# Adding x on TensorE in the attention that runs beside a causal convolution: identity product, ScalarE copy, VectorE scaling from the bank

## Chip, core and metric

The kernel runs on one core of a Trainium2 chip. The metric is the device time of one launch in microseconds. A core has TensorE (PE in the profile; PEld is its weight load), VectorE (DVE), ScalarE (ACT), GpSimd (POOL) and SyncE (SP), which only issues transfers here. Everything is in fp32, and each fp32 matmul of the program stands as two records in the trace.

## What is computed

The input x has 4 batches of 512 time steps with 128 x 64 = 8192 features each. Layer 0, cut to what matters here (`layernorm` runs over the 8192 features):

```python
xn = layernorm(x, ln_attn_g, ln_attn_b)
k, v, r = xn @ Wk, xn @ Wv, sigmoid(xn @ Wr)
states = scan(s -> decay * s + k_t * v_t)          # over time
x = x + (r * states) @ Wo                          # attention
xn = layernorm(x, ln_freq_g, ln_freq_b)
x = x + gelu(conv(xn, freq_W, 3 taps over the 128) + freq_b)
xn = layernorm(x, ln_time_g, ln_time_b)
to = causal_conv(xn, time_W, 3 taps over time, per feature) + time_b
x = x + layernorm(to, time_ln_g, time_ln_b)
x = x + gelu(x @ ffn_W1 + ffn_b1) @ ffn_W2 + ffn_b2
```

Layer 1 subtracts a moving average over time, takes 128 Fourier modes, mixes them by complex weights and adds the inverse transform to the average. The change does not touch it.

## The kernel before

Layer 0 keeps features on the 128 partitions and the 512 time steps along the free dimension. The 8192 features are 64 chunks of 128, taken in 32 pairs; nearly every tile of layer 0 is a pair, 128 x 2 x 512.

For one batch the steps are `project` (J), `scan` (Z), `attend_and_convolve` (A), `convolve_time` (C), `open_feed` (O) and `feed_forward` (F). Two batches run beside each other. The function `in_turn` advances two Python generators by hand-written shares and leads, and TensorE's order is exactly this program order (`manual_schedule` for TensorE). On the other engines a scheduler orders the instructions; each engine then takes its own list strictly in order. The pairs that matter are C of batch 0, 1, 2 beside A of batch 1, 2, 3. A of batch 0 runs beside J of batch 1.

Inside A, `attend(i)` handles pair i. It loads `xp` (x, transposed) and `wo_sb`, multiplies them with `rst` (r times the states) into the PSUM tile `a` (L487: two products of 64 rows, one for each chunk), adds xp to it on VectorE into `x1` (L489), and multiplies x1 by the row `rb` of reciprocal deviations into `z` (L493). `scaled` makes weights on ScalarE (L501). `convolve(i)`, which trails attend by two pairs, fills a PSUM tile `cv` (tags `c` and `m` in turn): the bias and the mean's term by four two-row products (L508), the neighbours in the convolution by up to four 64 x 64 products (L517), and the pair's own part by two full products (L522). Then come a gelu in place on ScalarE (L523), the sum with x1 on VectorE into `x2` (L525), a store of x2 by POOL (L526), and its square on ScalarE (L528). `add_up` sums x2 and the squares over the features on TensorE into `st` (L249, 32 columns each), three pairs behind attend. Tile `a` has one buffer of two banks, xp, x1 and wo_sb have three, z has four.

Inside C, for each pair, VectorE scales x2 (L580) and subtracts the mean's row into `xh` (L582), ScalarE makes the first tap and the bias (L585, one for each chunk), VectorE adds the other two taps (L589, four instructions), POOL fixes the first two columns (L593) and stores, ScalarE squares (L595), and `add_up` sums into `p` (also L249).

`ident` is a 128 x 128 identity that is there from the start, as the second operand of transposes.

Of the kernel before, what the change touches and what calls it, by code (L numbers as in the profile page):

```python
# [12 lines left out]
ALU = mybir.AluOpType  # L13
# [3 lines left out]
P = 128  # L17
T = 512
NF = 128
H = 64  # L20
# [59 lines left out]
def layer0(ctx, tc, dram, x, xt, vecs, wkvr, wo, wdec, wconv, fbias, w1, fb1, w2, fb2, x4):  # L80
# [4 lines left out]
    nc = tc.nc  # L85
# [17 lines left out]
    def two(pool, tag):  # L103
        return pool.tile([P, 2, SL], F32, tag=tag, name=tag)


    ident = const.tile([P, P], F32, name="ident")
# [40 lines left out]
    cgr = const.tile([P, NPR, H], F32, name="cgr")  # L148
# [9 lines left out]
    def neighbours(q, c):  # L158

        return (c - 1, q), (c + 1, 1 - q)  # L160

    def rows_of(q, d):

        return 1 - q if d < 0 else q
# [79 lines left out]
    def add_up(st, i, pair, squares, first, last):  # L244

        for j in range(2):
            for k, src in ((0, pair), (1, squares)):
                q = 2 * j + k
                nc.tensor.matmul(  # L249
                    st[32 * q : 32 * q + 32, :], lhsT=ones, rhs=src[:, j, :],  # L250
                    start=first, stop=last,
                )

    def finish(st, bank, tag):

        s_sb = rowp.tile([P, SL], F32, tag="s", name="s_sb")
        nc.scalar.copy(s_sb, st)
        yield CHAIN
        pm = bank()
        for t in range(NT):  # L260
            nc.tensor.matmul(
                pm[:, 2 * t : 2 * t + 2], lhsT=s_sb[:, t * P : (t + 1) * P], rhs=pick,
                start=True, stop=True,
            )
        me = tiny.tile([P, NT, 2], F32, tag=f"me{tag}", name="me")
        nc.vector.tensor_copy(me.rearrange("p t k -> p (t k)"), pm[:, 0 : 2 * NT])
        return me[:, :, 0], me[:, :, 1]

    def moments(mean, square, tag):

        var, rs, mrs = cols(f"var{tag}"), cols(f"rs{tag}"), cols(f"mrs{tag}")
        nc.vector.tensor_tensor(var, mean, mean, ALU.mult)
        nc.vector.tensor_tensor(var, square, var, ALU.subtract)
        rsqrt(rs, var)
        nc.vector.tensor_tensor(mrs, mean, rs, ALU.mult)
        return rs, mrs

    def rows(bank, a, b, names):
        both = rowp.tile([P, 2, SL], F32, tag=names, name=names)
        for k, col in enumerate((a, b)):  # L280
            pb = bank()
            spread(pb, col)
            nc.scalar.copy(both[:, k, :], pb)
            yield CHAIN
        return both[:, 0, :], both[:, 1, :]

    def pair_of(row):
        return row.unsqueeze(1).to_broadcast([P, 2, SL])

    def load_x(b, i):  # L290
        xp = fr.tile([P, 2, SL], F32, tag="xp", name="xp")
        nc.sync.dma_start(xp, xt[b, 2 * i : 2 * i + 2].rearrange("c p t -> p c t"))
        return xp

    def c_bank():
        return two(ps_c, "c")
# [174 lines left out]
    def attend_and_convolve(b):  # L471
        rst, rs, mrs = scanned.pop(b)
        rb, mb = yield from rows(of_a, rs, mrs, "rm")

        nc.vector.tensor_scalar(mb, mb, at_one[:, 1:2], at_one[:, 0:1], ALU.mult, ALU.add)
        st = ps_s.tile([P, SL], F32, tag="s", name="st")
        free_s[0] = False
        x1s, zs, ws, waiting = {}, {}, {}, {}

        def attend(i):  # L480
            xp = load_x(b, i)
            wo_sb = fr.tile([P, P], F32, tag="wo", name="wo_sb")
            nc.sync.dma_start(wo_sb, wo[:, i, :])
            at = two(ps_a, "a")
            for j in range(2):
                js = slice(j * S, (j + 1) * S)
                nc.tensor.matmul(at[:, j, :], lhsT=wo_sb[js, :], rhs=rst[js, :], start=True, stop=True)  # L487
            x1 = x1s[i] = fr.tile([P, 2, SL], F32, tag="x1", name="x1")
            nc.vector.tensor_tensor(x1, at, xp, ALU.add)  # L489
            z = fr.tile([P, 2, SL], F32, tag="z", name="z", bufs=4)  # L490
            for j in range(2):
                zs[2 * i + j] = z[:, j, :]
            nc.vector.tensor_tensor(z, x1, pair_of(rb), ALU.mult)  # L493

        def scaled(i):

            wcs = fr.tile([P, 2, P + H], F32, tag="wcs", name="wcs")
            for j in range(2):
                c = 2 * i + j
                ws[c] = wcs[:, j, :]  # L500
                nc.scalar.mul(wcs[:, j, :], wc_sb[:, i % 2, :], vec[:, G2, c : c + 1])  # L501

        def convolve(i):
            cv = c_bank() if i % 2 or held[0] else two(ps_m, "m")
            for h in range(2):
                for j in range(2):
                    q = 32 * (2 * h + j)
                    nc.tensor.matmul(  # L508
                        cv[h * H : (h + 1) * H, j, :], lhsT=cgr[q : q + 2, i, :], rhs=mb[q : q + 2, :],
                        start=True, stop=False,  # L510
                    )
            for j in range(2):
                c = 2 * i + j
                for n, h in neighbours(i % 2, c):
                    if 0 <= n < NCH:
                        rs = halves[rows_of(n // 2 % 2, n - c)]
                        nc.tensor.matmul(  # L517
                            cv[halves[h], j, :], lhsT=ws[n][rs, P:], rhs=zs[n][rs, :], start=False, stop=False
                        )
            for j in range(2):  # L520
                c = 2 * i + j
                nc.tensor.matmul(cv[:, j, :], lhsT=ws[c][:, 0:P], rhs=zs[c], start=False, stop=True)  # L522
            nc.scalar.activation(cv, cv, AF.Gelu_apprx_tanh)  # L523
            x2 = two(bk, "x2")
            nc.vector.tensor_tensor(x2, cv, x1s.pop(i), ALU.add)  # L525
            nc.gpsimd.dma_start(x2d[b][2 * i : 2 * i + 2].rearrange("c p t -> p c t"), x2)  # L526
            sq2 = bk.tile([P, 2, SL], F32, tag="sq", name="sq2")
            nc.scalar.activation(sq2, x2, AF.Square)  # L528
            for c in (2 * i - 2, 2 * i - 1):
                zs.pop(c, None)  # L530
                ws.pop(c, None)
            if i + 2 < NPR:
                scaled(i + 2)
            waiting[i] = x2, sq2

        for i in range(2):
            scaled(i)
        for i in range(NPR + 3):
            if i < NPR:
                attend(i)  # L540
                yield 1.0
            if 1 < i < NPR + 2:
                convolve(i - 2)
                yield 5.0
            if i > 2:
                add_up(st, i - 3, *waiting.pop(i - 3), i == 3, i == NPR + 2)
                yield 1.0
        begin[attend_and_convolve], free_s[0] = b + 1, True
        mean3, sq3 = yield from finish(st, of_a, 3)
        carried[b] = moments(mean3, sq3, 3)  # L550
# [503 lines left out]
```

## Time and profile before

| | |
|---|---|
| median of 3 runs | 3954.09 us (3950.18 to 3962.51) |
| profiled execution, its time and its span | 3956.46 us, 3954.4 us |
| busy: PE, PEld, DVE, ACT, POOL | 94%, 35%, 67%, 45%, 15% of the span |
| granted TensorE clock, mean | 0.974 |
| the three stretches of A beside C | about 588 to 860, 1285 to 1560, 1996 to 2285 us |
| DVE busy in them | 255.9, 262.6, 268.7 us |

How to read it: a group or timeline row names the line of the kernel, the engine, the operation and "output<-inputs" by tile names; tiles that share a name in the program share it there, so `x` in an attention row stands for xp, x1 or x2. The busy time of PE counts a matmul until its modelled end, so a PE that is "busy" can still be late for its next start. An idle time before an instruction is given with the instruction that ended it, its releaser.

### The profile page before, as it was taken

The page shows a single profiled execution, that of the slowest core. Times are in us where ns is not written, and L with a number is a line of the kernel's source. Part 1 is how long each engine was busy: PE and PEld are TensorE (multiplying, and loading weights), DVE is VectorE, ACT ScalarE, POOL GpSimd, SP SyncE. Part 2 cuts the span into 40 slices and gives each one's busy share as a digit, 9 for nine tenths or more (in the row PEclk, how much of TensorE's full clock was granted, in tenths as well). Part 3 has the DMA queues.
Part 4 walks back from the last instruction along what each step waited for, and adds up shares of the span by engine and source line. Part 5 has one row for each costly group of instructions (what it writes and reads, how often), then busy time and mean ns, then how long its engine had stood idle before and what let it go on. Part 6 is the DMA issues. An engine that isn't in the chain of part 4 may idle for free. (4 is left out here: it accounts for less than half of the span.)

```text
span 3954.4 us, 45957 instructions
## 1 busy us (share of the span) xinstructions
PE 3721.8 (94%) x16463; PEld 1373.1 (35%) x16463; DVE 2646.6 (67%) x3430; ACT 1761.0 (45%) x2460; POOL 580.8 (15%) x1038
## 2 busy tenths in 40 slices
PE   9989989889999899999999988999989999999999
PEld 4433322223333222333322232333322653326533
DVE  1145559985555898655589989955549357783577
ACT  2113335545556555455556578877752210022100
POOL 0000002220000222000022222100014200142000
PEclk9989989999999999999989999999989999999999
DMA  5367637776664677767567767745549469895597
GB/s 173 126 224 262 231 127 242 249 254 228 232 234 149 232 258 247 247 221 236 172 209 255 258 218 257 244 160 179 182 155 306 163 196 297 297 303 176 186 294 268
DMA packets 417466, 884.49 MB, mean 224 GB/s; under 512 B 35352, under 2 KB 85720, under 8 KB 413144
## 3 DMA queue, kind: packets, MB, share of 16 engines
q1 hardware_dynamic: 334848, 605.12, 47.1%
q0 software_dynamic: 79872, 274.77, 19.3%
q8 instruction: 131, 2.15, 0.2%
q10 hardware_dynamic: 2520, 1.67, 0.1%
q14 instruction: 95, 0.78, 0.1%
HBM read 612.93 MB, written 268.50 MB: 223 GB/s over the span
## 5 line engine op out<-in xcount | busy, mean ns | idle before, releaser
L650 PE MATMUL pa<-mid,w_sb 128*64 128x512 f32 x2048 | 499.9, 609 | 49.5 <-DVE x4t L655 49.3
L643 ACT ACTIVATE mid<-m,fb_sb 128x1024 f32<-128x1024 f32 x256 | 284.9, 1113 | 294.8 <-PE m L639 294.2
L655 DVE SCALAR_TENSOR_TENSOR x4t<-pa,fb_sb,x 128x512 f32<-128x512 f32 x252 | 188.0, 746 | 254.2 <-PE pa L650 254.1
L639 PE MATMUL m<-x,w_sb 64*128 64x512 f32 x1008 | 289.8, 648 | 1.4 <-ACT mid L643 0.9
L589 DVE SCALAR_TENSOR_TENSOR to<-xh,vec,to 128x512 f32<-128x512 f32 x384 | 277.2, 746 | 10.7 <-issue 6.8
L643 ACT ACTIVATE mid<-c,fb_sb 128x1024 f32<-128x1024 f32 x256 | 283.2, 1106 | 0.6 <-PE c L639 0.6
L639 PE MATMUL c<-x,w_sb 64*128 64x512 f32 x1008 | 262.4, 594 | 1.3 <-ACT mid L643 1.3
L650 PEld LDWEIGHTS pa<-mid,w_sb 128*64 128x64 f32 x2048 | 125.0, 136 | 392.7 <-issue 227.5
L361 PE MATMUL a<-xp,both 128*128 128x512 f32 x512 | 244.8, 605 | 6.4 <-DVE both L358 5.9
L249 PE MATMUL st<-x,ones 128*32 128x512 f32 x512 | 204.2, 613 | 35.3 <-DVE x L525 35.2
L922 PE MATMUL b<-xin,avg_sb 128*128 128x512 f32 x512 | 230.9, 593 | 3.0 <-DVE xin L928 3.0
L899 ACT COPY two<-a 128x512 f32<-128x512 f32 x64 | 37.5, 585 | 424.1 <-PE a L894 424.1
L358 DVE TENSOR_SCALAR both<-both,vec 128x192 f32<-128x192 f32 x192 | 53.3, 316 | 258.5 <-DMA both<-in_wkvr 208.5
L928 DVE TENSOR_TENSOR xin<-b,pm 128x512 f32<-128x512 f32 x256 | 159.1, 684 | 95.4 <-PE b L925 80.5
L675 POOL DMA_DIRECT2D x<-ob x64 | 48.9, 765 | 1056.3 <-ACT ob L671 986.5
L616 ACT ACTIVATE kd<-kd,vec 128x512 f32<-128x512 f32 x256 | 193.6, 809 | 4.3 <-DVE kd L608 4.2
L528 ACT ACTIVATE sq<-x 128x1024 f32<-128x1024 f32 x128 | 134.6, 1051 | 135.6 <-DVE x L525 135.3
L249 PE MATMUL st<-sq,ones 128*32 128x512 f32 x640 | 172.2, 615 | 21.0 <-ACT sq L528 20.0
L825 DVE TENSOR_TENSOR uv<-xin 128x1024 f32<-128x1024 f32 x128 | 156.1, 1225 | 49.8 <-PE a L839 32.0
L355 DVE BATCH_NORM_STATS2 stt<-both 128x6 f32<-128x512 f32 x192 | 124.4, 685 | 92.7 <-DMA both<-in_x 91.8
L487 PE MATMUL a<-rst,wo_sb 64*128 64x512 f32 x512 | 153.5, 678 | 34.7 <-DVE x L489 33.6
L595 ACT ACTIVATE sq<-to 128x1024 f32<-128x1024 f32 x96 | 101.3, 1055 | 188.9 <-POOL xh L581 183.4
(242 smaller groups left out, 6804.3 us busy)
## 6 DMA issues: line engine op xcount, KB each, us to landing
xp<-in_xt SPq DMA_DIRECT2D x256, 512.0 KB
xin<-x SPq DMA_DIRECT2D x128, 1024.0 KB
kx<-x SPq DMA_DIRECT2D x224, 512.0 KB
x<-x POOLq DMA_DIRECT2D x128, 512.0 KB, 4.7
kh<-to SPq DMA_DIRECT2D x128, 512.0 KB
x<-ob POOLq DMA_DIRECT2D x64, 1024.0 KB, 6.7
out<-xin POOLq DMA_DIRECT2D x64, 1024.0 KB, 7.3
both<-in_x SPq DMA_DIRECT2D x96, 512.0 KB
```

Source lines behind the costliest of these rows:

```text
L249: nc.tensor.matmul(st[32 * q : 32 * q + 32, :], lhsT=ones, rhs=src[:, j, :], start=first, stop=last,)
L361: nc.tensor.matmul(pa[:, k, :], lhsT=wq[:, j, k * P : (k + 1) * P], rhs=xp[:, j, :], start=first and j == 0, stop=last and j == 1,)
L487: nc.tensor.matmul(at[:, j, :], lhsT=wo_sb[js, :], rhs=rst[js, :], start=True, stop=True)
L589: nc.vector.scalar_tensor_tensor(to[:, j, :], xh[:, j, k : SL + k], vec[:, w, c], to[:, j, :], ALU.mult, ALU.add)
L616: tc.keep_in_program_order(nc.scalar.activation(d[:, j, :], d[:, j, :], AF.Identity, bias=vec[:, B4, c], scale=vec[:, G4, c]))
L639: nc.tensor.matmul(pm[:, h, :], lhsT=w1_sb[hs, m * P : (m + 1) * P], rhs=x3[hs, :], start=True, stop=True)
L643: nc.scalar.activation(mid, pm, AF.Gelu_apprx_tanh, bias=fb1_sb[:, m : m + 1])
L650: nc.tensor.matmul(pa[h * H : (h + 1) * H, :], lhsT=w2_sb[:, m, :], rhs=mid[:, h, :], start=(m == 0), stop=(m == 1),)
L655: nc.vector.scalar_tensor_tensor(x4t, pa, fb2_sb, x3s[c // 2][:, c % 2, :], ALU.add, ALU.add)
L825: nc.vector.tensor_tensor(t, xin[:, 0:2, :], xin[:, 2:4, :], op)
L922: nc.tensor.matmul(po[j], lhsT=avg_sb[:, j, :], rhs=xin[:, j, :], start=True, stop=False)
L928: nc.vector.tensor_tensor(by_n(xin[:, j, :]), by_n(po[j]), by_c(pm[j % 2][:, j // 2, :]), ALU.add)
```

## The change

For batches 1, 2 and 3, attend(i) no longer adds xp on VectorE. TensorE adds it: a product of the identity with xp is accumulated onto `a`, for each of the two chunks. ScalarE then copies the sum from PSUM into x1, and VectorE reads the sum from PSUM, not from x1, to make z. Batch 0 keeps the old form. For all batches, the order of products inside convolve is turned round: the pair's own part first, then the neighbours, then the bias.

```diff
-                nc.tensor.matmul(at[:, j, :], lhsT=wo_sb[js, :], rhs=rst[js, :], start=True, stop=True)
+                nc.tensor.matmul(at[:, j, :], lhsT=wo_sb[js, :], rhs=rst[js, :], start=True, stop=b == 0)
             x1 = x1s[i] = fr.tile([P, 2, SL], F32, tag="x1", name="x1")
-            nc.vector.tensor_tensor(x1, at, xp, ALU.add)
+            if b == 0:
+                nc.vector.tensor_tensor(x1, at, xp, ALU.add)
+                base = x1
+            else:
+
+                for j in range(2):
+                    nc.tensor.matmul(at[:, j, :], lhsT=ident, rhs=xp[:, j, :], start=False, stop=True)
+                nc.scalar.copy(x1, at)
+                base = at
             z = fr.tile([P, 2, SL], F32, tag="z", name="z", bufs=4)
             for j in range(2):
                 zs[2 * i + j] = z[:, j, :]
-            nc.vector.tensor_tensor(z, x1, pair_of(rb), ALU.mult)
+            nc.vector.tensor_tensor(z, base, pair_of(rb), ALU.mult)
...
             cv = c_bank() if i % 2 or held[0] else two(ps_m, "m")
-            for h in range(2):
-                for j in range(2):
-                    q = 32 * (2 * h + j)
-                    nc.tensor.matmul(
-                        cv[h * H : (h + 1) * H, j, :], lhsT=cgr[q : q + 2, i, :], rhs=mb[q : q + 2, :],
-                        start=True, stop=False,
-                    )
+            for j in range(2):
+                c = 2 * i + j
+                nc.tensor.matmul(cv[:, j, :], lhsT=ws[c][:, 0:P], rhs=zs[c], start=True, stop=False)
...
-            for j in range(2):
-                c = 2 * i + j
-                nc.tensor.matmul(cv[:, j, :], lhsT=ws[c][:, 0:P], rhs=zs[c], start=False, stop=True)
+            for h in range(2):
+                for j in range(2):
+                    q = 32 * (2 * h + j)
+                    nc.tensor.matmul(
+                        cv[h * H : (h + 1) * H, j, :], lhsT=cgr[q : q + 2, i, :], rhs=mb[q : q + 2, :],
+                        start=False, stop=True,
+                    )
```

## Prediction, made before the changed kernel ran

> **What bounds the kernel now.** I read the page's busy line first. PE is busy for 94% of the span, but a matmul record includes its pipelined tail, so this alone does not show that PE sets the pace where the change is made. The changed branch runs only where attention of batch b stands beside the causal convolution of batch b-1. The busy time by windows of three such stretches of 50 us (PE, PEld, DVE, ACT, POOL busy, then granted clock, DMA share, GB/s) says who does:
>
> ```profile
> core 0: us, PE busy (x) PEld busy (x) DVE busy (x) ACT busy (x) POOL busy (x), PEclk, DMA share, GB/s
> 1400.00:1450.00 50.00, 45.33 (x228) 10.81 (x220) 50.00 (x56) 30.24 (x42) 12.61 (x24) 1.00 0.74 249
> 1450.00:1500.00 50.00, 46.10 (x235) 11.14 (x233) 49.86 (x54) 28.11 (x39) 13.98 (x23) 1.00 0.81 268
> 1500.00:1550.00 50.00, 45.59 (x233) 10.46 (x229) 49.48 (x53) 29.63 (x41) 14.77 (x22) 1.00 0.77 259
> ```
>
> VectorE (DVE) is busy without a gap; ACT has 40% free. The groups of DVE, one row per line and form, give its bill for one pair of chunks:
>
> ```profile
> L589 DVE SCALAR_TENSOR_TENSOR to<-xh,vec,to 128x512 f32<-128x512 f32 x113 | 82.5, 746 | 3.8 <-issue 2.7 <-ACT to L585 0.8
> L582 DVE TENSOR_TENSOR xh<-kd,rm 128x1024 f32<-128x1024 f32 x30 | 36.6, 1220 | 0.3
> L580 DVE TENSOR_TENSOR kd<-kx,rm 128x1024 f32<-128x1024 f32 x30 | 36.6, 1219 | 0.1
> L493 DVE TENSOR_TENSOR z<-x,rm 128x1024 f32<-128x1024 f32 x27 | 32.9, 1219 | 0.0
> L489 DVE TENSOR_TENSOR x<-a,xp 128x1024 f32<-128x1024 f32 x27 | 32.9, 1219 | 0.0
> ```
>
> L489, L493, L525, L580, L582 at 1.22 us and four L589 at 0.746 make 6.10 + 2.98 = 9.08 us. The measured period agrees: 11 L489 in each 100 us, 9.09 us. So DVE sets it.
>
> What does PE need for a period if it waits for nothing? The timeline of PE where attention of batch 0 runs beside a projection shows the same groups back to back; the start of each less the start of the one before is its price (start, us, operation):
>
> ```profile
> 407.06 1.13 PE L487 MATMUL a<-rst,wo_sb 64*128 64x512 f32 x4
> 408.12 1.98 PE L361 MATMUL m<-xp,both 128*128 128x512 f32 x4
> 410.04 1.09 PE L508 MATMUL c<-rm,cgr 2*64 2x512 f32 x8
> 411.06 1.09 PE L517 MATMUL c<-z,wcs 64*64 64x512 f32 x8
> 412.07 1.98 PE L522 MATMUL c<-z,wcs 128*128 128x512 f32 x4
> 413.89 1.88 PE L361 MATMUL m<-xp,both 128*128 128x512 f32 x4
> 415.70 0.62 PE L249 MATMUL st<-x,ones 128*32 128x512 f32 x1
> ```
>
> L487 1.06, L508 1.02, L517 1.01, L522 1.82; the sums of one statistic (8 records of L249) 1.00, from the next start at 416.70. A full 128x128 pair of products (L361) costs 1.92 behind another array shape, 1.81 behind its own. With two statistics a period is 1.06 + 1.02 + 1.01 + 1.82 + 2.0 = 6.9 us, so PE has about 2.2 us of slack, spent in waits for DVE and ACT, as in this timeline (bracket: idle before, and its releaser):
>
> ```profile
> 1401.95 1.22 DVE L525 TENSOR_TENSOR x<-c,x 128x1024 f32<-128x1024 f32 x1
> ...
> 1403.20 1.06 ACT L528 ACTIVATE sq<-x 128x1024 f32<-128x1024 f32 x1 [3.63 <-DVE x L525]
> ...
> 1403.22 1.05 PE L249 MATMUL st<-x,ones 128*32 128x512 f32 x2 [0.83 <-DVE x L525]
> ```
>
> A hand-over costs little: L528 starts 0.03 us after L525 ends.
>
> **What the Trainium skill says.** (1) VectorE: DVE Perf Modes, "The perf-mode tier table": a fp32 tensor_tensor runs in the 1x tier from SBUF and PSUM alike. The trace agrees: L489 (one input in PSUM) and L493 (both in SBUF) both take 1.219 us, so the scaling costs the same when it reads the bank. (2) PSUM — Partial Sum Buffer, "Terms": two engines must not touch one bank and quadrant at once, "reads against reads included". So copy and scaling can't run together; no line of before has such a pair, but in the changed program as built the scaling waits for ScalarE. (3) TensorEngine Tiling (Array Packing), "Key Properties": a change of tiling mode drains TensorE. The trace fits: 1.92 against 1.81. (4) TensorE: Matmul & The Clock Gate, "What's actually happening": activity releases the half-rate clock, idling brings it back. The windows of before show clock 1.00 above, but 0.92 over the third such stage (1996 to 2285 us).
>
> **The change part by part**, for 3 batches x 32 = 96 pairs:
>
> - *Removed:* L489 on DVE, 1.22 us. DVE is left with 7.86 us a period.
> - *Added on PE:* two products of 128x128 with the identity, in four records: like L361 behind L487, 1.92 us. They wait for xp, which DVE waited for before; same loads, same queue order at the start, and xp is freed by PE.
> - *Added on ACT:* a copy of 128x1024 from PSUM. The same operation at L369 took 1.012 us. ACT goes from 1.00 + 1.06 + 0.80 + 1.60 + 1.05 = 5.5 to 6.5 us a period: no bound by its sum.
> - *Moved:* in convolve the product L522 comes first and the bias L508 last, for batch 0 too. The number of array-shape changes is the same where L361 stands on either side, and next to the identity product one is saved: 0 for batch 0, from -0.1 to +0.1 us elsewhere. No DMA, POOL work or buffer count changes.
>
> *PE's new period:* 1.06 + 1.92 + 1.82 + 1.02 + 1.01 + 1.85 to 2.0 for the two statistics (1.85 if adjacent, from 1413.76 to 1415.61 in the timeline) = 8.7 to 8.8; I take 8.75. It exceeds DVE's 7.86, so **PE becomes the bound** and the best gain is 9.08 - 8.75 = 0.33 us, not 1.22.
>
> *Waits in the changed order.* The scheduler orders DVE and ACT; I took these orders from the changed program as built. In about 56 of the 96 periods DVE runs x2 (old L525), the four causal multiply-adds, the shift (L582), then the scaling: 4.2 us between x2 and the scaling, in which ACT does the square, half of L585 and the copy. The loop through ACT (x2 1.22, square 1.06, L585 0.80, two multiply-adds 1.49, three DVE operations 3.66, hand-overs 0.1) is 8.3 us, under 8.75. These gain 0.33 x 56 = **-18 us**.
> In 6 periods x2 stands directly ahead of the next scaling, which waits for the copy, which waits in ACT's order behind the square, which waits for x2. Then DVE stands still through both: 7.86 + 1.06 + 1.01 + hand-overs 0.05 = 9.98, or 0.9 more than now: **+6**.
> In 9 periods ACT also has the other square (L595, 1.05) in the loop: 8.3 + 1.05 = 9.4, 0.3 more: **+3**.
> The other 25 are ramps and changes of order. At a stage's start three attends run ahead of the first convolution. Today bank a is free after L489 alone (L487 starts at 1285.17, 1289.45, 1291.90); afterwards it takes 3.0 on PE, 1.01 copy, 1.22 scaling, so 5.3 us each: two gaps of 5.3 against 6.7 in all is +4, and up to +13 at half clock (products 6.0 instead of 3.0). I take +8 x 3 stages = **+24**. Where attention runs alone (some 3 periods, not counting starts) PE already sets the pace, 541.32 - 535.31 = 6.0 us, and the 1.92 counts in full: **+6**.
> *Clock.* At clocks 0.98, 0.98, 0.92 over 272, 275 and 289 us, half speed covers about 11 + 11 + 46 = 68 us (a mean of 0.98 is 4% of the time at half), which PE's slack mostly hides now; a PE-bound stage would lose half, 34 us. But a busier PE should fall there less: bounds 0 to +34, I take **+5**.
>
> Sum: -18 + 6 + 3 + 24 + 6 + 5 = +26. The profiled execution is 3956.5 us, its span 3954.4; the median of the runs is 3954.1, 0.06% away, so I add to the median: **3980 us** (+0.65%).
>
> **Rivals.**
> - *A, forecast: PE takes over and ramps lose more than the steady part gains.* For it: the PE bill above. Against: the -18 is sure only if the clock holds. Its own range is 3966 to 4010. Chance 0.45.
> - *B, the serial hand-over rules most periods:* when a transfer or slow clock upsets the order, every period runs through x2, square, copy, scaling. 96 x 0.9 = +86, 4040. For it: ACT and DVE take their work strictly in order. Against: only 6 periods stand so by order. Chance 0.20.
> - *C, faster:* DVE frees PE from its waits and the ramps are covered by causal work that DVE now does ahead. Price: 96 x -0.33 = -32, so 3922; it decides if each stage's start costs under 2 us rather than 8 and the clock stays at 1. For it: DVE is at 50.00 of 50. Against: the PE floor allows no more. Chance 0.15.
> - *D, both cancel,* ramps near +4 and clock at 0: within 12 us. Chance 0.20. The copy or product not being issued is no case: both stand in the changed program's lists, 96 times.
>
> **How the numbers follow.** About 0.3% (12 us) is what a measurement of this kernel can tell from no change. C gives faster 0.15, D same 0.20, A and B slower 0.65. The range leaves the further half of C and of B's upper tail out: 3940 to 4040.
>
> **What would show it.** Right: in the three stages DVE has gaps ahead of the scaling and the copy, PE is near 8.7 us a period with hardly an idle time before L249, the copy is near 1.01 and the scaling near 1.22 us, the first three attends of a stage stand 5 us or more apart. Wrong: a period still at 9.1 with DVE full; an identity pair well under 1.9 us; periods of 10 us through most of a stage (B); starts no later than today (C).

## The result and the profile after

The changed kernel takes 3975.98 us (median of 4 runs, 3971.61 to 3981.31), the kernel before 3953.41 us beside it (4 runs). The ratio is 1.0054, 95% interval 1.0033 to 1.0075: slower by about half a per cent. The profiled execution took 3981.31 us, its span is 3979.5 us, 25.1 us longer than the span before.

The changed kernel has other line numbers: the scaling L493 is now L501, the copy is L496 and the identity product L495; in convolve the pair's own part is L515, the neighbours L521, the bias L527, the gelu L531, x2 L533 and its square L536; in the causal convolution L588, L590, L593, L597 and L603 stand for the old L580, L582, L585, L589 and L595. The layer 1 line L825 is L833. The kernels of the experiments shift these numbers again; there the tile names tell what a row is.

The busy line of the page after:

```profile
PE 3800.9 (96%) x16847; PEld 1428.1 (36%) x16847; DVE 2562.9 (64%) x3334; ACT 1859.9 (47%) x2556; POOL 600.4 (15%) x1038
```

The work moved as the diff says: VectorE lost 84 us of busy time, ScalarE got 99, PE got 79. The prices of the new operations, first copy and scaling by line (count; ns of the shortest, the median and the longest; first and last start), then the group of the identity product (busy us and mean ns of one record; idle before):

```profile
L496 ACT COPY x<-a x96: 986/993/1014, 562.5 to 2280.3; 128x1024 f32<-128x1024 f32 x96
L501 DVE TENSOR_TENSOR z<-a,rm x96: 1214/1218/1225, 563.6 to 2281.3; 128x1024 f32<-128x1024 f32 x96
...
L495 PE MATMUL a<-xp,ident 128*128 128x512 f32 x384 | 198.7, 642 | 0.0
```

The scaling costs the same from the bank, and PE was never idle ahead of the identity product, so it never waited for xp.

The busy time by windows of the three stretches of attention beside the causal convolution, as in the table of before:

```profile
core 0: us, PE busy (x) PEld busy (x) DVE busy (x) ACT busy (x) POOL busy (x), PEclk, DMA share, GB/s
588.00:862.00 274.00, 266.01 (x1360) 80.86 (x1357) 236.06 (x259) 191.91 (x251) 83.16 (x129) 0.99 0.72 245
1287.00:1575.00 288.00, 274.89 (x1350) 80.28 (x1352) 236.30 (x251) 188.25 (x248) 72.40 (x123) 0.99 0.70 238
2006.00:2300.00 294.00, 280.96 (x1400) 84.26 (x1398) 239.47 (x259) 196.73 (x251) 85.90 (x128) 0.97 0.69 239
```

PE is now the fullest engine (266.0 of 274 us in the first stage, against 242.5 of 272 before), VectorE has 38 us free where it had 16, and the granted clock is 0.99, 0.99, 0.97 where it was 0.98, 0.98, 0.92.

**Where the time went.** I laid the two profiles against each other from one scaling to the next. "Starts" are the first two gaps between scalings of each of the three stages, "rest" is from the third scaling of a stage to its last:

| | before | after | difference |
|---|---|---|---|
| starts, three stages | 6.3 + 5.9 + 7.7 | 14.2 + 14.1 + 18.5 | +26.9 |
| rest, three stages | 261.8 + 259.4 + 259.2 | 260.2 + 261.6 + 252.3 | -6.3 |
| all else of layer 0 | | | -1.4 |
| layer 1, code untouched (first L825 or L833 to the end) | 1000.4 | 1006.3 | +5.9 |

Layer 0 ends 19.2 us later. Layer 1 took from 996.7 to 1006.8 us over the profiles of this case with the same code, so its 5.9 us are no part of the change. The gain of the rest is small and uneven: the first two stages are together 0.6 us longer than before and the third, where the clock had been lowest, is 6.9 us shorter. The loss is in the starts. The timeline after at the first of them (start, us, engine, operation; bracket: idle before, and its releaser):

```profile
559.40 1.13 PE L487 MATMUL a<-rst,wo_sb 64*128 64x512 f32 x4 [0.68 <-ACT rm L283]
...
560.47 1.98 PE L495 MATMUL a<-xp,ident 128*128 128x512 f32 x4
...
562.53 1.01 ACT L496 COPY x<-a 128x1024 f32<-128x1024 f32 x1 [3.18 <-PE a L495]
563.57 1.22 DVE L501 TENSOR_TENSOR z<-a,rm 128x1024 f32<-128x1024 f32 x1 [3.64 <-ACT x L496]
...
564.85 1.13 PE L487 MATMUL a<-rst,wo_sb 64*128 64x512 f32 x4 [2.40 <-DVE z L501]
...
565.91 3.68 PE L495 MATMUL a<-xp,ident 128*128 128x512 f32 x4
...
569.67 1.01 ACT L496 COPY x<-a 128x1024 f32<-128x1024 f32 x1 [6.13 <-PE a L495]
570.72 1.23 DVE L501 TENSOR_TENSOR z<-a,rm 128x1024 f32<-128x1024 f32 x1 [5.92 <-ACT x L496]
...
572.00 1.29 PE L487 MATMUL a<-rst,wo_sb 64*128 64x512 f32 x4 [2.40 <-DVE z L501]
```

The reader is to see a chain without a second buffer: the product of wo_sb with rst, the identity product, the copy, the scaling, and only then the next product, because all four work on the one tile `a`. From product to product it takes 5.45 us the first time and 7.15 the second. The second time the identity product takes 3.68 us instead of 1.98: PE had been idle for 2.40 us, and the clock granted from 566.02 to 569.42 us is 0.50. All six identity products inside the gaps of the three starts are slow like this, 2.94 to 3.68 us.

PE had nothing else to do in its own order, where the first convolution stands behind the third attend. By its data it needs only the first two pairs; an order that sets it ahead was not tried.

Away from the starts PE sets the pace. PE's rows of one period:

```profile
692.56 1.13 PE L487 MATMUL a<-rst,wo_sb 64*128 64x512 f32 x4
...
693.62 1.98 PE L495 MATMUL a<-xp,ident 128*128 128x512 f32 x4
...
695.44 1.88 PE L515 MATMUL c<-z,wcs 128*128 128x512 f32 x4
...
697.25 1.09 PE L521 MATMUL c<-z,wcs 64*64 64x512 f32 x8
...
698.27 1.09 PE L527 MATMUL c<-rm,cgr 2*64 2x512 f32 x8
...
701.14 1.13 PE L487 MATMUL a<-rst,wo_sb 64*128 64x512 f32 x4
```

Start less start: L487 1.06, L495 1.82, L515 1.81, L521 1.02, L527 1.01, the two statistics 1.86, in all 8.58 us without a wait. In 46 of the 87 periods of the rest one L487 follows the other after 8.6 us; the mean of all 87 is 8.9. What PE waited for from 590 to 840 us, in the kernel before (three rows) and in the changed one (the last row; releaser, us in total, times, longest):

```profile
PE st L249 <- DVE x L525: 11.4, 10, 3.9
PE st L249 <- ACT sq L528: 9.2, 15, 1.3
PE a L487 <- DVE x L489: 3.0, 6, 1.3
```

```profile
PE a L487 <- DVE z L501: 4.4, 5, 1.7
```

The waits ahead of the sums (L249) are gone. In the rest of all three stages PE's bill, 87 times 8.58, is 746 of 774 us; before, with the prediction's 6.9, it was 600 of 780. PE's idle times over 0.06 us, added up there, fell from 69.1 to 15.9 us, and VectorE's rose from 35.9 to 101.1. The serial loop that the prediction described is there too, in 6 periods of the second stage:

```profile
1392.62 1.22 DVE L533 TENSOR_TENSOR x<-c,x 128x1024 f32<-128x1024 f32 x1
...
1393.87 1.06 ACT L536 ACTIVATE sq<-x 128x1024 f32<-128x1024 f32 x1 [3.88 <-DVE x L533]
...
1394.84 0.99 ACT L496 COPY x<-a 128x1024 f32<-128x1024 f32 x1
...
1395.86 1.23 DVE L501 TENSOR_TENSOR z<-a,rm 128x1024 f32<-128x1024 f32 x1 [2.02 <-ACT x L496]
```

x2, its square, the copy and the scaling follow each other with 0.03 us between them at most; VectorE stands still for 2.02 us, and the next x2 comes at 1402.42, 9.80 us after this one.

### The profile page after: what moved, and what is told of

The parts are those of the page before. It is cut to its first block, busy times and chain, and to the rows that moved or that the text cites. A ratio compares the mean times of both kernels' runs of the same rounds, so it can differ in the third digit from the quotient of the medians.

```text
span 3979.5 us, 46600 instructions
## 1 busy us (share of the span) xinstructions
PE 3800.9 (96%) x16847; PEld 1428.1 (36%) x16847; DVE 2562.9 (64%) x3334; ACT 1859.9 (47%) x2556; POOL 600.4 (15%) x1038
## 3 DMA queue, kind: packets, MB, share of 16 engines
q0 software_dynamic: 79872, 274.77, 19.3%
## 5 line engine op out<-in xcount | busy, mean ns | idle before, releaser
L658 PE MATMUL pa<-mid,w_sb 128*64 128x512 f32 x2048 | 500.1, 609 | 45.5 <-DVE x4t L663 45.4
L597 DVE SCALAR_TENSOR_TENSOR to<-xh,vec,to 128x512 f32<-128x512 f32 x384 | 283.5, 749 | 50.4 <-ACT to L593 44.2
L361 PE MATMUL a<-xp,both 128*128 128x512 f32 x512 | 243.5, 602 | 6.4 <-DVE both L358 5.9
L536 ACT ACTIVATE sq<-x 128x1024 f32<-128x1024 f32 x128 | 134.9, 1054 | 187.7 <-DVE x L533 187.2
L495 PE MATMUL a<-xp,ident 128*128 128x512 f32 x384 | 198.7, 642 | 0.0
L833 DVE TENSOR_TENSOR uv<-xin 128x1024 f32<-128x1024 f32 x128 | 156.3, 1224 | 51.6 <-PE a L847 30.1
L487 PE MATMUL a<-rst,wo_sb 64*128 64x512 f32 x512 | 149.9, 663 | 38.1 <-DVE z L501 33.2
L858 ACT COPY xf<-a 128x512 f32<-128x512 f32 x128 | 73.5, 630 | 236.8 <-PE a L854 236.8
L672 PEld LDWEIGHTS pt<-ident,x4t 128*128 128x128 f32 x1024 | 107.5, 141 | 207.9 <-ACT mid L651 161.5
```

Source lines behind the costliest of these rows:

```text
L361: nc.tensor.matmul(pa[:, k, :], lhsT=wq[:, j, k * P : (k + 1) * P], rhs=xp[:, j, :], start=first and j == 0, stop=last and j == 1,)
L495: nc.tensor.matmul(at[:, j, :], lhsT=ident, rhs=xp[:, j, :], start=False, stop=True)
L597: nc.vector.scalar_tensor_tensor(to[:, j, :], xh[:, j, k : SL + k], vec[:, w, c], to[:, j, :], ALU.mult, ALU.add)
L658: nc.tensor.matmul(pa[h * H : (h + 1) * H, :], lhsT=w2_sb[:, m, :], rhs=mid[:, h, :], start=(m == 0), stop=(m == 1),)
L833: nc.vector.tensor_tensor(t, xin[:, 0:2, :], xin[:, 2:4, :], op)
```

## Experiments

Theory T: the starts carry the loss, because the bank now passes through three engines in turn; in the rest PE's bill takes the place of VectorE's for a small gain. Rivals put the loss on the turned order of products, on the copy's place in ScalarE's list, or on the identity product wherever it stands. The gaps given below are again "starts" and "rest" of the three stages. In the diffs, "-" and "+" are against the kernel that is named.

**1. The order alone.** The kernel before, with convolve's products in the changed kernel's order (own part, neighbours, bias: all of the change's diff in convolve) and nothing else. One line of it, which moves to the front:

```diff
 # against before, in convolve(i)
-                nc.tensor.matmul(cv[:, j, :], lhsT=ws[c][:, 0:P], rhs=zs[c], start=False, stop=True)
+                nc.tensor.matmul(cv[:, j, :], lhsT=ws[c][:, 0:P], rhs=zs[c], start=True, stop=False)
...
```

> Only the turned order of products inside convolve (own part, neighbours, bias); attend is that of the kernel before, for all batches. Theory T (TensorE's longer bill and the three slower stage starts carry the loss): the order is worth nothing beside the causal convolution, where VectorE sets 9.09 us a pair, and the 3 us by which batch 0's attention ended earlier in the changed kernel: 3948 to 3956 us. Rival U (the order of products carries a good part of the loss): 3960 us or more.

3947.99 us (22 runs) against 3950.91; ratio 0.9992 (0.9983 to 1.0002). Starts 4.9, 6.1, 7.7. The order alone is worth nothing that can be told from noise, as forecast. The rest of the stages is 778.1 us here against 780.4 in the kernel before, so some 2 us between two profiles mean nothing.

**2. The old form for the first three pairs of a stage.**

```diff
 # against after, in attend(i)
-... start=True, stop=b == 0)
+... start=True, stop=b == 0 or i < 3)
-            if b == 0:
+            if b == 0 or i < 3:
```

> The changed kernel, but pairs 0, 1 and 2 of each batch add xp on VectorE as before; identity product and copy from pair 3 on. Theory T: the first two gaps between scalings fall from 7.1 us (11.1 and 7.3 in the third stage) back to about 3, which takes off 20 to 27 us: 3950 to 3956 us, no slower than the kernel before. Rival S (the hand-over from the copy to the scaling loses the time in every period, and starts only shift it): no more than 8 us come back, 3968 us or more.

3953.60 us (22 runs) against 3950.91; ratio 1.0005 (0.9995 to 1.0014). The loss is gone, as T expected. Starts are back at 4.9, 5.9, 7.7; the rest is 259.1, 263.5, 255.5 us, 778.0 in sum, between the changed kernel (774.1) and the kernel before (780.4). PE's rows at the first start show why:

```profile
561.98 1.13 PE L487 MATMUL a<-rst,wo_sb 64*128 64x512 f32 x4 [0.68 <-ACT rm L283]
564.43 1.13 PE L487 MATMUL a<-rst,wo_sb 64*128 64x512 f32 x4 [1.33 <-DVE x L490]
566.89 1.13 PE L487 MATMUL a<-rst,wo_sb 64*128 64x512 f32 x4 [1.33 <-DVE x L490]
```

The bank is free again after 2.45 us instead of 5.45 and 7.15. Nine of 96 pairs carry the whole loss, and the other 87 win nothing that the times can tell.

**3. No identity product.** The copy and the scaling from the bank stay; x is not added in batches 1 to 3.

```diff
 # against after, in attend(i)
-                for j in range(2):
-                    nc.tensor.matmul(at[:, j, :], lhsT=ident, rhs=xp[:, j, :], start=False, stop=True)
                 nc.scalar.copy(x1, at)
```

> The changed kernel without the identity product: xp is loaded and never added (left out of the sum); the copy by ScalarE and the scaling from the bank stay. Theory T: TensorE's bill falls from 8.6 to 6.8 us a pair, so VectorE (7.86) or its loop through ScalarE (8.3) sets the period: 0.3 to 0.6 us less than 8.6 in some 70 periods, and 1.8 us less in each of two gaps at three starts (3.6 at half clock): 3925 to 3945 us. Rival S (the copy and its hand-over set the new period, not the product): within 8 us of the changed kernel, 3968 to 3984 us.

3932.78 us (6 runs); ratio 0.9951 (0.9932 to 0.9970), so about 1.0% below the changed kernel, where T expected it. Starts 9.0, 8.6, 8.9; the rest 253.3, 246.9, 237.5. Without the product the changed form gains, so neither copy nor scaling sets the pace of most periods. The starts stay longer than before: copy and scaling are still one behind the other. The rest is 42.7 us shorter than before, much more than the time shows. In the profiled execution 19.7 us of this are lost between the first and the second stage, where VectorE waits once for 24.0 us for the weights of a projection to arrive; whether the product's absence brings this about is not known.

**4. The identity product, and VectorE's add kept.** No copy; x is added twice in batches 1 to 3. The order of convolve is turned.

```diff
 # against before, in attend(i); convolve as in 1
+            if b > 0:
+                for j in range(2):
+                    nc.tensor.matmul(at[:, j, :], lhsT=ident, rhs=xp[:, j, :], start=False, stop=True)
             nc.vector.tensor_tensor(x1, at, xp, ALU.add)
```

> The turned order, and the identity product as in the changed kernel, but VectorE still adds xp (so xp is in the sum twice) and scales from x1; no copy. Theory T: TensorE's 8.6 us stay under VectorE's 9.08, so the steady part is that of the kernel before; a start costs 1.8 us more for each of two gaps (3.6 at half clock) in three stages, and the stretches where attention runs alone 6 us: 3962 to 3974 us. Rival S (the copy does the harm, TensorE hides its product): 3948 to 3958 us. Rival V (TensorE's product lengthens every period although its sum is under VectorE's, because its waits don't shrink): 3990 us or more.

4005.89 us (5 runs); ratio 1.0142 (1.0119 to 1.0165). T missed by over 30 us. Starts 8.7, 8.7, 11.4 (+8.9 in all); the rest 281.2, 275.9, 272.4 (+49). Of its 87 periods 38 take 9.0 us, with VectorE idle for 0.38 us in each, and 8 take 10.0 us. VectorE's rows in one of the long ones (L528 is x2 here, L592 the multiply-adds):

```profile
1494.57 1.22 DVE L528 TENSOR_TENSOR x<-c,x 128x1024 f32<-128x1024 f32 x1
1495.70 1.53 DVE L592 SCALAR_TENSOR_TENSOR to<-xh,vec,to 128x512 f32<-128x512 f32 x2
1498.56 0.75 DVE L592 SCALAR_TENSOR_TENSOR to<-xh,vec,to 128x512 f32<-128x512 f32 x1 [1.33 <-ACT to L588]
```

VectorE waits for the second tap of ScalarE (L588), which stands in ScalarE's list behind the square of x2 and the square of `to`. So the product does cost something although VectorE, with the add, has as many instructions as before. V's figure was met, but not for V's reason: PE's waits did shrink (its bill of 746 us leaves 83 of 829.5, where 180 were left before), and in the 9.0 us periods VectorE is nearly full. Runs 9 and 10 take this up.

Runs 3 and 4 also split the starts. Copy and scaling alone lengthen them by 6.6 us, the product alone by 8.9, both together by 26.9. Most of the difference is the slow clock: five of the six identity products in the starts of run 4 take 1.98 us, none in the changed kernel. By these rows I estimate that the slow clock makes up 11 of the 26.9 us (8.3 in the identity products, 2.6 in L487).

**5. The old order of products in the changed kernel.** Bias, neighbours, own part again; one line of it, which moves back to the end:

```diff
 # against after, in convolve(i)
-                nc.tensor.matmul(cv[:, j, :], lhsT=ws[c][:, 0:P], rhs=zs[c], start=True, stop=False)
+                nc.tensor.matmul(cv[:, j, :], lhsT=ws[c][:, 0:P], rhs=zs[c], start=False, stop=True)
...
```

> The changed attend (identity product, copy, scaling from the bank) with the order of products in convolve that the kernel before had (bias, neighbours, own part). Theory T (the order is worth nothing): within 6 us of the changed kernel's +0.54% to the kernel before, 3966 to 3980 us beside 3951 to 3954 for the kernel before. Rival U (the turned order is needed to feed TensorE with scalings that come later): 3985 us or more.

3984.57 us (6 runs); ratio 1.0086 (1.0069 to 1.0103). Above what T expected, and next to the rival's figure. PE's rows of one period:

```profile
697.06 1.13 PE L487 MATMUL a<-rst,wo_sb 64*128 64x512 f32 x4
698.12 1.98 PE L495 MATMUL a<-xp,ident 128*128 128x512 f32 x4
700.03 1.09 PE L516 MATMUL c<-rm,cgr 2*64 2x512 f32 x8
701.05 1.09 PE L525 MATMUL c<-z,wcs 64*64 64x512 f32 x8
702.07 1.98 PE L530 MATMUL c<-z,wcs 128*128 128x512 f32 x4
703.98 0.62 PE L249 MATMUL p<-to,ones 128*32 128x512 f32 x1
...
705.84 0.70 PE L487 MATMUL a<-rst,wo_sb 64*128 64x512 f32 x2
```

(L516 is the bias here, L525 the neighbours, L530 the own part.) The period is 8.78 us, 0.2 more than in the turned order: the full products cost 1.91 each where they stand apart, and 1.82 and 1.81 where one follows the other. One change of array shape more in each period comes to 0.2 us. The rest of the stages is only 5.4 us longer than in the changed kernel, and the intervals of the two ratios overlap, so beside the identity product the turned order is worth some 5 us by the profiles and 13 by the ratios, hardly clear of noise, and nothing without it (run 1).

**6. The scaling ahead of the copy.**

```diff
 # against after, in attend(i)
-                nc.scalar.copy(x1, at)
                 base = at
...
             nc.vector.tensor_tensor(z, base, pair_of(rb), ALU.mult)
+            if base is at:
+                nc.scalar.copy(x1, at)
```

> The changed kernel with two lines exchanged: the scaling from the bank stands ahead of the copy, so the copy waits for the scaling. Theory T (in the second stage the periods of 9.8 us are the loop x2, square, copy, scaling): no period of 9.8 us is left there, since the copy is off that loop. In the other periods the copy now stands ahead of the gelu on ScalarE and behind the scaling, a loop of 8.8 us (x2 1.22, square 1.06, tap 0.80, two taps 1.49, scaling 1.22, copy 1.0, weights 0.8, gelu 1.0, hand-overs 0.2) against 8.6: 3966 to 3984 us in all, starts as slow as in the changed kernel. Rival W (those periods of 9.8 us come from something else, the POOL fix or the order of the second statistic): they stay at 9.8 us.

3997.09 us (5 runs); ratio 1.0116 (1.0098 to 1.0134): worse than the changed kernel, where T expected much the same. The 9.8 us periods are gone, as T said, but in their place stand periods of 9.1 and 10.1 us in turn, and T's loop of 8.8 us is there as 8.69 us in 40 of 87 periods. PE waits for the copy, and VectorE for a tap behind it:

```profile
1401.21 0.99 ACT L502 COPY x<-a 128x1024 f32<-128x1024 f32 x1
...
1402.25 1.13 PE L487 MATMUL a<-rst,wo_sb 64*128 64x512 f32 x4 [0.54 <-ACT x L502]
...
1404.58 1.54 DVE L598 SCALAR_TENSOR_TENSOR to<-xh,vec,to 128x512 f32<-128x512 f32 x2 [1.66 <-ACT to L594]
```

The bank's last reader is now ScalarE, whose list is in strict order, so the wait moved from VectorE to PE: 19.3 us before L487 in the rest of the stages, and VectorE's waits for taps grew from 41.4 to 62.5 us. Turning the two readers round did not shorten the hand-over here; it changed who stands in it.

**7 and 8. Sharing the adds.** Both keep the old form for the first three pairs. In run 7 every third pair has the old form as well, in run 8 every second.

```diff
 # against after, in attend(i); run 7, then run 8 (the stop flag likewise)
+            if b == 0 or i < 3 or i % 3 == 0:
+            if b == 0 or i < 3 or i % 2 == 0:
```

> As the run with the old start (pairs 0, 1, 2 old), and besides every third pair (i divisible by 3) adds xp on VectorE; copy ahead of the scaling as in the changed kernel. Theory T (the bound is what is left after the work is shared out): TensorE's mean bill is 8.6 - 0.6 = 8.0 us and VectorE's 7.86 + 0.41 = 8.27, so the mean period falls from 8.6 to about 8.3 where no loop through ScalarE is longer: 3930 to 3946 us, faster than the kernel before. Rival S (periods are set by loops through ScalarE and by the scheduler's order, not by the sums): 3950 us or more.

> As the previous one, but every second pair adds xp on VectorE. Sums a pair: TensorE 8.6 - 0.9 = 7.7, VectorE 7.86 + 0.61 = 8.47. Theory T: a mean period of 8.5, so slower than with two of three, 3936 to 3952 us. Rival S: no order between the two, 3950 us or more.

Run 7: 3947.57 us (14 runs), ratio 0.9993 (0.9983 to 1.0003), not faster than before, between the figures of T and S. Run 8: 3936.62 us (12 runs), ratio 0.9970 (0.9959 to 0.9980): **faster than both kernels**, by 0.3% and, by the ratios, 0.8%. T's figure for run 8 was met, but T had the two the other way round, so it does not explain them; S, with no order between the two and 3950 us or more, failed as well. In 36 of run 8's 87 periods the gaps alternate between 10.1 and 6.6 us, 8.4 by the mean, but part of the second stage has 9.1 and 9.8 us in turn, and the mean over all is 8.9. The rest of its stages is 776.0 us in sum, 4.4 less than before, so a third of its gain stands there; the profile of one execution doesn't place the remainder.

**9 and 10. The product with the add, without ScalarE's second square; and the control.** In run 9 the kernel of run 4 has the square of `to` replaced by a fill, and in run 10 the kernel before has the same. The second statistic of `to` is left out in both.

```diff
 # run 9 against run 4; run 10 against before
-                nc.scalar.activation(sq, to, AF.Square)
+                nc.gpsimd.memset(sq, 1.0)
```

> As the run with both the product and VectorE's add, and besides ScalarE no longer squares the causal result: POOL fills that tile with ones, so the second statistic is wrong (left out). Theory L (that run's periods of 10 us are a loop in which a tap waits in ScalarE's order behind two squares): with one square gone and the two taps ahead of the other, VectorE's waits for a tap (13.5 us in the second stage) go below 3 us and the run is 20 us or more faster than with the square: 3960 to 3985 us. Rival V (TensorE's longer bill lengthens the periods): within 8 us of that run's 4006 us.

> The kernel before with the same square left out (POOL fills the tile with ones), as the control of the run before: there VectorE waits for a tap 0.8 us in the second stage, so both theories expect no gain, within 8 us of the kernel before: 3943 to 3959 us.

Run 9: 3968.26 us (6 runs), ratio 1.0051 (1.0032 to 1.0070), 38 us below run 4. L's figure was met, and VectorE's waits for a tap in the second stage fell to 2.7 us, as L said; V failed. Run 10: 3930.63 us (6 runs), ratio 0.9951 (0.9933 to 0.9969), where no gain was expected. So about half of what run 9 gained is no matter of run 4's loop. Run 9 is still 1.0% slower than its control: in 33 of its 87 periods L487 follows L487 after 8.6 us, PE's bill, which is so in only 3 periods of run 4. To see why the control gained, I added up VectorE's records from the third scaling of each stage to its last: their durations; the overlap, by which an instruction starts before the one ahead has ended; and the idle times over 0.06 us (what is left over, up to 8 us, are starts just behind the end):

| kernel | length | durations | overlap (times) | idle |
|---|---|---|---|---|
| before | 780.4 | 806.3 | -62.7 (749) | 35.9 |
| after | 774.1 | 694.8 | -29.9 (361) | 101.1 |
| 4, product and add | 829.5 | 809.6 | -45.4 (543) | 59.0 |
| 9, the same, no square | 788.2 | 806.8 | -53.4 (662) | 31.0 |
| 10, before, no square | 760.5 | 802.5 | -60.1 (777) | 17.6 |

Before, VectorE stood idle for 35.9 us of these 780, and run 10 takes 18.3 of it away: that is most of its gain. The control's forecast failed since I took VectorE for full all through, from windows in which it was. Run 4's 49 us over the kernel before are 23 us of idle, 17 us of overlap that got lost, and 9 us of the remainder. The square accounts for 28 us of the idle time of run 4, but also for 18 in the control. What makes the overlap go is in the section on the hardware.

## Why the prediction was right

It said 3980, range 3940 to 4040, and slower at 0.65; measured is 3975.98. The mechanism, PE taking over and the starts losing more than the rest gains, is what runs 2 and 3 and the idle times of PE show. That the sum came within 4 us is in part luck, because some of its terms were off in opposite directions. By its steps:

- **Starts, +24 forecast, +26.9 measured.** Run 2 puts them back and the loss is gone: shown by an edit. The mechanism was right, the size was a choice between a full-clock and a half-clock case. (The half-clock case of +13 counts three slow products; two gaps make +10.) Measured are 7.9, 8.2 and 10.8 us a stage, with the identity products at 2.94 to 3.68 us instead of 1.98.
- **PE becomes the bound at 8.75 us, measured 8.58.** The mis-sized term is the identity pair, taken at 1.92 "behind another array shape"; another 128x128 product follows it, and it took 1.82. The prediction's own rows had such a case: L522 stands behind the 64x64 products and ahead of L361, and cost 1.82. Only a pair of products that stands alone between other shapes cost 1.91 or 1.92. For the turned order the prediction gave -0.1 to +0.1 us and took the middle, 0.
- **VectorE's period 9.08: the step that was wrong.** It added durations, and the sum fitted the period by chance. VectorE was full in the windows that the prediction shows, but not over the whole stages. VectorE's instructions start 1.13 and 0.66 us apart where they last 1.22 and 0.75, so its five and four make 8.3 us; the measured period of 8.97 (780.4 over 87 gaps) also holds 0.41 of idle (35.9 over 87) and some pairs of the causal convolution more than of the attention. The difference that the forecast used survived, because both terms were too high: the 50 periods after that are like the 56 it counted take 8.53 us by the mean, the periods at the same places before 8.88, which makes -17 us against -18.
- **The 6 serial periods, +6 forecast, +2.6 measured**: 9.80 us instead of 9.98, and 9.37 before, not 9.08 (6 times 0.9 is 5.4, besides). **The 9 with the other square, +3 forecast, -1.0 measured**: 8.97 us; the bill of 9.4 added 1.05 for a square that was mostly hidden.
- **Attention alone, +6 forecast, +5.1 measured.** From the fourth L487 of each stage to the fifth PE took 6.0 us before and 7.7 after, in three periods as forecast. By the gaps between scalings the 16 periods at the ramps, these among them, are 6.1 us longer, and 6 periods that change from one order to another are 3.2 us longer, which had no term.
- **Clock, +5 forecast.** Outside the starts a busier PE kept its clock, as the windows above show (0.97 in the third stage against 0.92); no run separates what that was worth.
- **"The order of products is worth 0"** held in the kernel before (run 1) and probably not beside the identity product (run 5), where it saves 5 to 13 us, hardly clear of noise.

Where did the add's time go? VectorE was spared 111.5 us of durations in the rest of the stages (806.3 to 694.8). 65 us came back as idle time, 33 us as lost overlap and 7 us as starts just behind an end; 6 us are left. The waits of VectorE in the second stage after (engine and line, releaser, us in total, times, longest) name the idle time:

```profile
DVE z L501 <- ACT x L496: 18.9, 8, 5.8
DVE to L597 <- ACT to L593: 15.4, 19, 1.3
```

These rows are from 1300 to 1570 us, and the longest wait for the copy, 5.8 us, still belongs to the start. Over the rest of all three stages 41 of the 101 us are waits for ScalarE's taps, 35 for the copy and 19 for the gelu. This is how a VectorE that is no longer the bound looks. The Trainium skill, Perfetto Trace Analysis, "Optimizing Scalar/DVE Operations", says that moving work to ScalarE may make sense where VectorE is saturated; in this case the path did not go to ScalarE alone, it also needed 1.82 us of PE, and PE had too little room for all 96 pairs. With 45 pairs moved (run 8) neither engine is full: PE's idle times in the rest are 58.6 us, VectorE's 50.7.

What stays open: why the scheduler orders VectorE otherwise once the product is added (run 4), why run 8 is faster than run 7, and where two thirds of run 8's gain lie. The slow clock's part in the starts is an estimate; no run keeps the chain and changes the clock.

## What to carry to other kernels

Work taken from a full engine gains only down to the back-to-back bill of the next one, so add up that engine's starts, not durations, before moving all of it. Here, with the starts left in the old form, moving 45 pairs gained 0.3% and moving 87 gained nothing; moving all 96 lost 0.5%. Price the filling of a stage apart from its steady part: a single-buffered bank that is written for longer and read by two engines in turn instead of one cost 27 us in six gaps, where the 87 other periods won 6 at most. A longer chain can also leave PE idle long enough to lose its clock, which the estimate above puts at 11 of the 27. A change of readers or order on a strictly ordered engine can move waits to whoever is behind it, as in run 6, so each of these wants its own run.

## What the runs showed of the hardware

**Overlap on VectorE depends on the order.** Four causal multiply-adds, first in the kernel before and then in the changed one, from VectorE's timeline:

```profile
1399.30 2.73 DVE L589 SCALAR_TENSOR_TENSOR to<-xh,vec,to 128x512 f32<-128x512 f32 x4
1401.95 1.22 DVE L525 TENSOR_TENSOR x<-c,x 128x1024 f32<-128x1024 f32 x1
1403.08 1.21 DVE L582 TENSOR_TENSOR xh<-kd,rm 128x1024 f32<-128x1024 f32 x1
```

```profile
1397.00 2.98 DVE L597 SCALAR_TENSOR_TENSOR to<-xh,vec,to 128x512 f32<-128x512 f32 x4
```

In the first, L582 starts 1.13 us after L525, which lasts 1.22. The Trainium skill, Perfetto Trace Analysis, "Optimizing Scalar/DVE Operations", says that the write acknowledgement in an instruction's profiled time overlaps with the next instruction. The records show such an overlap, about 0.084 us each (62.7 us in 749 places before), though not what overlaps. But where an instruction needs what the one directly ahead writes, it starts some 0.03 us behind its end: so did all nine scalings of the kernel before that stand right behind the add of their x1. In the second row two of the four steps are such (the two multiply-adds of one chunk back to back), and the four take 2.98 us instead of 2.73. In the kernel before 7 multiply-adds follow one another like that within the stages, in the changed kernel 151, in run 4 126. A sum of durations is therefore too high by about 0.08 us for each instruction that does not need the one directly ahead; the more of a list does, the nearer the sum comes.
